# Halves of the neighbours' sums stored tile by tile, and step 1's adjacency products placed anew, in a four-layer graph kernel

## The chip, the cores and the metric

The kernel runs on one core of a Trainium2 chip. The metric is device time in microseconds (us) of one execution; less is better. The kernel before has a median of 3286.2 us over 14 runs (3276.45 to 3298.38).

Five engines work side by side, each through its own queue in order: TensorE (PE; matmuls, its weight loads shown as PEld), VectorE (DVE), ScalarE (ACT), GpSimd (POOL) and SyncE (SP). DMAs are issued from the queues of SP, ACT and POOL. They wait for one another by semaphores.

## What is computed

The input is x (4096 x 256) and a symmetric 0/1 adjacency `adj` (4096 x 4096, about 33 entries in a row). Four layers follow one another, each with a residual and a layer norm. The change lies in the second, which makes two steps:

```python
R = S + jnp.eye(N); R = R / R.sum(-1, keepdims=True)      # S is adj
Xf = X; Xa = X
for n in range(STEPS):                                    # two steps
    A = _top_p_attention(Xa, W1, W2, W3)                  # softmax, kept up to mass 0.9, normalised
    Xf = R @ Xf
    Xa = A @ Xa
    Z = Z + Xf @ U1[n].T + Xa @ U2[n].T
h = X + Z                                                 # then a layer norm
```

`R @ Xf` is the neighbours' sum: an adjacency product, a row sum and a scale. `A @ Xa` is attention. Layers one, three and four have one adjacency product each; the third also needs the number of two-way edges of each row.

## The kernel before

All rows are cut into 32 tiles of 128. Values that must keep their precision go through TensorE as two halves, an upper one of the leading bits and the rest; `split` (L145) makes them with three operations: L148 (VectorE, mask), L149 (ScalarE, copy of the upper half) and L150 (VectorE, subtraction). An adjacency product of one tile is 32 matmuls 128x512 over the halves of all tiles (`xh`, one buffer of the pool's tag "H") and one more for the diagonal (L683, L685 in `neighbours`); the adjacency comes as 8-bit pieces from `adj8_d` over SP's queue (L678) and is cast by ScalarE (L680). `r_end` (L700) scales the sum (L702, L703) and stores it in `xf_d` (L709). In step 0 the same loop also makes the two-way edge counts (L693, read at L707).

`run_step` (L941) is called for step 0 and step 1. Its loop runs i from -2 to 31. Iteration i makes the logits of tile i + 2 (L411, L412), searches the largest entries of tile i + 1 (L430, L525, L527), and multiplies tile i by its attention, then mixes (L819, L821). In step 0 a row keeps at most 16 entries: GpSimd gathers them (L669) and TensorE sums them (L758) with diagonal tiles (L756). In step 1 the whole row is turned (L741) and multiplied (L766). `pieces` (L720) runs the eight groups of a tile, and puts four matmuls of an adjacency product into each group if the iteration has one. Before the loop's first tile (i < 0) products are made by themselves (`r_product`, L711).

Which product belongs to which iteration: `FIRST` lists, for each step, the products of i = -2 and i = -1; each later iteration i makes product i + 2, if that is beyond FIRST's last. In step 0 that is 0 to 1, 2 to 3, then one in each iteration up to i = 29. In step 1, products 0 to 4 are made in the boundary between the steps (L1050), 5 to 7 in i = -2, 8 to 10 in i = -1, and 11 to 31 in i = 9 to 29, so that iterations 0 to 8 have none.

Rows whose kept mass needs more entries than were searched are set aside and done in extra tiles, "jobs" (`put_off`, L894): one in step 0, four in step 1, begun at i = 7, 15, 23 and 30 and moved on twice in each iteration, with five probes of a whole row (L495) in step 1. `left_over` (L921) is a loop for those beyond the jobs; all engines read its trip count (L926), which makes a barrier of it. In step 0 it stands in the last iteration. Behind the step's loop come the boundary's products, then `finish` of the job, whose flag (L585) is read back for a branch (L645).

The halves that step 1 needs are made in step 0's last iteration by `load_halves` (L152, called at L1026): eight loads of four tiles from `xf_d` over SP's queue into a scratch tile (the buffer of a logits tile), each followed by a split.

The order on each engine is not the order of the source: a scheduler of the framework arranges the instructions between two branches on each engine's queue. It already puts matmuls of later products ahead into iterations that have none. The text below calls the result the planned order; for the changed program it can be listed without running it.

Of the kernel before, what the change touches and what calls it, by code (L numbers as in the profile page):

```python
# [11 lines left out]
F32 = mybir.dt.float32  # L12
I32 = mybir.dt.int32
# [4 lines left out]
F32R = mybir.dt.float32r  # L18
# [6 lines left out]
P = 128  # L25
D = 256
# [28 lines left out]
def gnn_stack(ctx, tc, x, adjt, adjn, w0, b0, w1, w2t, w3t, u1t, u2t, ln_g, ln_b, w2, b2, w3, b3, out):  # L55
# [3 lines left out]
    nc = tc.nc  # L59
    N = x.shape[0]  # L60
    NT = N // P
    LC = min(512, N)
    NLC = N // LC
    JP = min(8, NT)
# [50 lines left out]
    zu_d = dram.tile([N + P, 2 * D], F32, name="zu_d")  # L115
    xa_d = dram.tile([N + P, D], F32, name="xa_d")
    xf_d = dram.tile([N, D], F32, name="xf_d")
    list_d = [dram.tile([N + P, 1], I32, name=f"list{n}_d") for n in range(STEPS)]

    adj8_d = [dram.tile([P, NT, P], F8, name=f"adj8_{it}_d") for it in range(NT)]  # L120
# [8 lines left out]
    def rows(t, it):  # L129
        return t[it * P : (it + 1) * P, :]  # L130

    def all_rows(t):
        return t.rearrange("(t p) d -> p t d", p=P)
# [18 lines left out]
    def load_halves(scratch, src, queue, cols=slice(None), ahead=2, copy=nc.scalar.copy):  # L152


        xh = hpool.tile([P, NT, 2 * D], F32R, tag="H", name="xh")
        W = J0 * D
        for c in range(NT // J0):
            s = slice(c * J0, (c + 1) * J0)
            t, up = (scratch[:, k * W : (k + 1) * W].rearrange("p (j d) -> p j d", d=D) for k in (c % ahead, ahead + c % 2))
            if queue is None:  # L160
                t = src[:, s, :]
            else:
                queue.dma_start(t, all_rows(src)[:, s, cols])
            split(up.bitcast(I32), xh[:, s, :], t, copy)
        return xh
# [186 lines left out]
    with tc.tile_pool(name="l1", bufs=1, reuse_waits="tile") as l1:  # L352
# [2 lines left out]


        FIRST = [[range(k * NT // 16, (k + 1) * NT // 16) for k in range(2)]]
        FIRST.append([range(5 * NT // 32, 8 * NT // 32), range(8 * NT // 32, 11 * NT // 32)])
        ones_sq = l1.tile([P, P], F32, name="ones_sq")
        nc.vector.memset(ones_sq, 1.0)  # L360

# [71 lines left out]
        QW = N // NQ  # L433

        spare_row = l1.tile([P, 4 * QW], U8, name="spare_row")
        no_e = spare_row[:, 4 * P : 4 * P + QW]

        def sparse(st):

# [260 lines left out]
        def r_end(i, acc_r, pn):  # L700
            xf_new = work.tile([P, D], F32, tag="xf_new", name="xf_new", bufs=1)
            nc.scalar.activation(xf_new, acc_r[:, :D], AF.Copy, scale=rs[:, i : i + 1])  # L702
            nc.vector.scalar_tensor_tensor(xf_new, acc_r[:, D:], rs[:, i : i + 1], xf_new, op0=ALU.mult, op1=ALU.add)  # L703
            if pn is not None:

                junk = spare_row.bitcast(F32)[:, :P]
                nc.vector.scalar_tensor_tensor(junk, pn[:, :P], 1.0, ident, op0=ALU.mult, op1=ALU.mult,  # L707
                                               accum_out=nef[:, i : i + 1])
            nc.sync.dma_start(rows(xf_d, i), xf_new)  # L709

        def r_product(n, i, xf):  # L711

# [228 lines left out]
        def run_step(n, es):  # L941

            later = {"base": spare0}
            tiles = {}
            last = []
            jobs = []

            def advance(job):  # L950

                cur["late"] = True
                st = next(job["stages"], "end")
                cur["late"] = False
                if st == "end":
                    return True
                if st is not None:
                    job["st"] = st
                return False

            def finish(job, last, todo=(), beside=()):
                while not advance(job):
                    for f in todo[:4]:
                        f()
                    todo = todo[4:]
                for f in todo:
                    f()
                ops = {}
                for k, f in enumerate(beside):
                    ops.setdefault(k * NLC // len(beside), []).append(f)  # L970
                for k, fs in enumerate(last):
                    ops.setdefault(k + 1, []).extend(fs)
                cur["late"] = True
                pieces(n, job["st"], None, ops)
                cur["late"] = False
                return [[f] for f in after(n, job["st"])]

            starts = {min((k + 1) * NT // LATER[n] - 1, NT - 2): k for k in range(LATER[n])}
            for i in range(-2, NT):
                st = tiles.pop(i, None)  # L980
                cd = tiles.get(i + 1)
                nxt = None
                if i + 2 < NT:

                    nxt = {"tile": i + 2, "q": cur["qs"].pop(0), "e": logits_in(es[i % 2]), "later": later, "G": {}}
                    tiles[i + 2] = nxt
                if i + 1 == NT and n == 0:
                    for fs in last:
                        for f in fs:
                            f()  # L990
                    last = []
                    left_over(n, es[NT % 2], later)
                ops = {}

                def at(g, f, *args):
                    ops.setdefault(g, []).append(lambda: f(*args))

                for g, fs in zip((1, 2), last):
                    for f in fs:
                        at(g, f)  # L1000
                if 0 < i + 2 < NT - 1:
                    turned = []
                    g = 1 if n else 6
                    at(g - 1, lambda i, turned: turned.append(transposed(cur["xa"][:, i + 3, :])), i, turned)
                    at(g, lambda turned: cur["qs"].append(query(None, turned[0])), turned)
                if cd is not None:
                    peak_groups(cd)
                    at(1, exp_rows, cd)
                for job in jobs:
                    at(1, advance, job)  # L1010
                if cd is not None:
                    rounds = 8 if n else KEPT // 8
                    at(2, tops, cd, rounds)
                    at(2, pick, cd, rounds)
                    at(4, flag, cd)
                    if n == 0:
                        for k in range(8):
                            at(4 + k // 2, gather, cd, k)
                    else:
                        at(5, lambda cd: [None for _ in settle(cd)], cd)  # L1020
                for job in jobs:
                    if n and i + 1 == NT:
                        at(4, advance, job)
                    at(6, advance, job)
                if i + 1 == NT and n == 0:
                    cur["next"] = load_halves(es[1 - NT % 2], xf_d, nc.sync)  # L1026
                if i < 0:
                    now = FIRST[n][i + 2]
                else:
                    now = [i + 2] if FIRST[n][1][-1] < i + 2 < NT else []  # L1030
                pieces(n, st, nxt, ops, now)
                last = [[f] for f in after(n, st)] if st is not None else []
                if i in starts:
                    k = starts[i]
                    if len(jobs) > (i == NT - 2):
                        last = finish(jobs.pop(0), last)
                    e = es[NT % 2] if k + 1 == LATER[n] else es[2]
                    jobs.append({"stages": put_off(n, k, e, later)})
                    if i < NT - 2:
                        advance(jobs[-1])  # L1040
            if n == 0:
                for fs in last:
                    for f in fs:
                        f()
                last = []
                cur["late"] = True
                fetch(n, jobs[0]["st"])
                cur["late"] = False
                cur["nef_done"] = True
                for i in range(FIRST[1][0][0]):  # L1050
                    r_product(1, i, cur["next"])
            todo = []
            if n > 0:

                z_room(es[1 - NT % 2])
                todo = [lambda i=i: zu_tile(i) for i in range(NT)]
            for k, job in enumerate(jobs):
                if k + 1 < len(jobs):
                    last = finish(job, last, beside=todo[: NT // 2])
                    todo = todo[NT // 2 :]  # L1060
                else:
                    last = finish(job, last, todo)
            for fs in last:
                for f in fs:
                    f()
            if n > 0:
                left_over(n, es[NT % 2], later)

        for n in range(STEPS):
            cur["n"] = n  # L1070
# [155 lines left out]
```

## Time and profile before

| what | us |
|---|---|
| median of 14 runs | 3286.2 |
| lowest, highest | 3276.45, 3298.38 |
| the profiled execution | 3294.68 |
| its span, first to last instruction | 3293.0 |
| TensorE busy in the span | 2976.4 (90%) |
| VectorE busy | 2291.4 (70%) |
| ScalarE busy | 1743.7 (53%) |
| GpSimd busy | 788.5 (24%) |

The stages in the span: layer one up to about 370 us, step 0 with its first products up to 1262, the boundary to 1418, step 1 to 2743, layers three and four to the end.

How to read the rows: a group of instructions shows its line, engine, operation, output<-inputs, shape and number, then busy time, mean ns of one, and the idle time of the engine just before them with what ended it. A timeline row shows start, length, engine, line, operation, tile, number of instructions, and in brackets the idle time before it and its releaser. A busy TensorE is not TensorE at its peak, since matmuls are pipelined and their ends are modelled. A wait for several semaphores is put down to the one that came last.

### The profile page before, as it was taken

How to read it: one execution, taken by the hardware profiler on the slowest of the kernel's cores; microseconds unless marked ns; L12 is line 12 of the kernel's file. 1: busy time of each engine (PE TensorE's matmuls, PEld its weight loads, DVE VectorE, ACT ScalarE, POOL GpSimd, SP SyncE). 2: the span in 40 equal slices, each digit the busy share in tenths (PEclk: the TensorE clock that was granted, in tenths of full speed). 3: DMA queues.
4: the chain of work that ended last, by engine and by line, in shares of the span. 5: the costliest groups of instructions: out<-in, count | busy, mean ns of one | idle time of the engine just before them, and what ended most of it. 6: DMA issues, size and time to landing. Idle time of an engine off the chain costs nothing. (4 is left out here: it accounts for less than half of the span.)

```text
span 3293.0 us, 45754 instructions
## 1 busy us (share of the span) xinstructions
PE 2976.4 (90%) x14376; PEld 2337.7 (71%) x14376; DVE 2291.4 (70%) x7161; ACT 1743.7 (53%) x2906; POOL 788.5 (24%) x915
## 2 busy tenths in 40 slices
PE   7999878999999996889989898989999796999998
PEld 3788656777777774668877777777787654888886
DVE  4666767787777885367988897888799673444444
ACT  3555545565555663465555454545465333666664
POOL 1111256666666664000000001000100001000000
PEclk9999989999999998989999999999999898999999
DMA  9995457777777775140001111011011134333332
GB/s 169 163 176 106 81 103 130 127 149 136 134 125 137 132 143 147 45 136 26 25 23 23 31 39 31 25 33 34 26 39 27 48 135 127 109 107 105 104 108 82
DMA packets 247872, 300.14 MB, mean 91 GB/s; under 512 B 34688, under 2 KB 201536, under 8 KB 247616
## 3 DMA queue, kind: packets, MB, share of 16 engines
q0 software_dynamic: 46576, 104.94, 23.1%
q1 hardware_dynamic: 188800, 180.93, 18.6%
q10 hardware_dynamic: 12240, 11.23, 1.1%
q8 instruction: 116, 1.90, 0.2%
q14 instruction: 140, 1.15, 0.2%
HBM read 331.17 MB, written 66.45 MB: 121 GB/s over the span
## 5 line engine op out<-in xcount | busy, mean ns | idle before, releaser
L683 PE MATMUL acc_r<-xh,adjq 128*128 128x512 f32 x2048 | 612.4, 430 | 39.2 <-ACT adjq L680 22.2
L766 PE MATMUL acc_bank<-xa,at 128*128 128x256 f32 x2304 | 570.3, 388 | 34.4 <-ACT at L744 33.9
L669 POOL DMA_INDIRECT G<-x_d,cols x512 | 500.0, 977 | 292.5 <-PE acc_bank L758 118.8
L680 ACT CAST adjq<-adj 128x512 fp32r<-128x512 fp8e4 x512 | 316.3, 620 | 404.6 <-PE acc_r L683 197.3
L766 PEld LDWEIGHTS acc_bank<-xa,at 128*128 128x128 f32 x2304 | 425.2, 194 | 96.3 <-ACT at L744 45.0
L683 PEld LDWEIGHTS acc_r<-xh,adjq 128*128 128x128 f32 x2048 | 377.8, 192 | 138.7 <-ACT adjq L680 49.2
L412 ACT COPY e<-lg 128x512 f32<-128x512 f32 x552 | 320.4, 587 | 241.6 <-PE lg L411 201.2
L430 DVE MAX8 cand<-e 128x8 f32<-128x256 f32 x1024 | 383.1, 415 | 74.7 <-ACT e L412 42.7
L197 POOL TENSOR_TENSOR rstd<-ve,mhalf 128x1 f32<-128x1 f32 x168 | 103.4, 615 | 1352.7 <-DVE ve L195 1287.9
L411 PE MATMUL lg<-kS,q 128*128 128x512 f32 x1104 | 401.6, 449 | 10.8 <-issue 5.4
L1106 ACT CAST a<-a 128x1024 fp32r<-128x1024 fp8e4 x256 | 267.9, 1048 | 157.5 <-PE acc L173 121.3
L758 PE MATMUL acc_bank<-G,dg 128*128 128x256 f32 x1024 | 286.8, 399 | 38.2 <-DMA G<-x_d,cols 15.9
L527 DVE FIND_INDEX8 cols<-top,e 128x8 uint32<-128x4096 f32 x64 | 282.8, 4419 | 0.0
L173 PE MATMUL acc<-xh,a 128*128 128x512 f32 x1024 | 255.7, 403 | 21.6 <-DMA a<-adj_d 15.8
L758 PEld LDWEIGHTS acc_bank<-G,dg 128*128 128x128 f32 x1024 | 196.6, 197 | 93.5 <-DMA G<-x_d,cols 26.5
L173 PE MATMUL acc<-y0h,a 128*128 128x512 f32 x1024 | 253.7, 400 | 0.0
L173 PEld LDWEIGHTS acc<-xh,a 128*128 128x128 f32 x1024 | 191.6, 190 | 64.9 <-ACT xh L149 24.1
L173 PE MATMUL acc<-yh,a 128*128 128x512 f32 x1024 | 233.7, 390 | 0.0
L744 ACT COPY at<-at_ps 128x512 f32<-128x512 f32 x296 | 173.7, 589 | 101.5 <-PE at_ps L741 100.2
L173 PEld LDWEIGHTS acc<-yh,a 128*128 128x128 f32 x1024 | 192.1, 188 | 39.7
L173 PEld LDWEIGHTS acc<-y0h,a 128*128 128x128 f32 x1024 | 188.0, 188 | 42.2 <-issue 0.6
L411 PEld LDWEIGHTS lg<-kS,q 128*128 128x128 f32 x1104 | 185.8, 195 | 34.5 <-ACT e L412 13.4
(287 smaller groups left out, 4519.4 us busy)
## 6 DMA issues: line engine op xcount, KB each, us to landing
adj<-adj_d SPq DMA_DIRECT2D x256, 128.0 KB
a<-adj_d SPq DMA_DIRECT2D x256, 128.0 KB
a<-in_adjt POOLq DMA_DIRECT2D x64, 256.0 KB
adj_d<-a SPq DMA_DIRECT2D x64, 256.0 KB
adjn<-in_adjn POOLq DMA_DIRECT2D x64, 256.0 KB
x_d<-x SPq DMA_DIRECT2D x64, 128.0 KB
xf_d<-xf_new SPq DMA_DIRECT2D x64, 128.0 KB
G<-x_d,cols POOLq DMA_INDIRECT x512
```

What stands on the lines that cost most here:

```text
L173: nc.tensor.matmul(acc, a[:, j, :], halves(jt), start=(jt == 0), stop=(jt == NT - 1))
L411: nc.tensor.matmul(pl[:, :LC], q[k], kS[:, s], start=(k == 0), stop=(k == 1))
L412: nc.scalar.copy(l[:, s], pl[:, :LC])
L430: nc.vector.max(dst[:, 8 * g : 8 * g + 8], src[:, g * GW : (g + 1) * GW])
L527: nc.vector.max_index(st["at"][:, 8 * r : 8 * r + 8], t8, st["e"][:, :N])
L669: nc.gpsimd.indirect_dma_start(out=g, out_offset=None, in_=x1_d, in_offset=bass.IndirectOffsetOnAxis(ap=st["at"][:, k : k + 1], axis=0))
L680: nc.scalar.copy(a, cur["a8"][:, g % 2 * GP : (g % 2 + 1) * GP, :])
L683: nc.tensor.matmul(acc_r, a[:, j, :], xf[:, jt, :], start=(jt == 0), stop=False)
L744: nc.scalar.copy(at[:, :G, :], ps[:, :G, :])
L758: nc.tensor.matmul(acc_a, dg[:, k % 4, :], st["G"][k], start=(k == 0), stop=(k == KEPT - 1))
L766: nc.tensor.matmul(acc_a, ats[g][:, j, :], cur["xa"][:, jt, :], start=(jt == 0), stop=(jt == NT - 1))
L1106: nc.scalar.copy(a, a8)
```

## The change

A new tensor `xh_d` (4096 x 512) in device memory takes the halves. In step 0, `r_end` splits each tile's sum as soon as it is made (L148 to L150 on one tile, 128x256, through a strip of `spare_row`) and stores the halves over SP's queue; `xf_d` is stored as before. The exponentials' unused output `no_e` moves behind that strip. `load_halves` at the end of step 0 is replaced by four loads of eight tiles each, straight into the operand, issued behind iteration 29. The scratch tile is no longer used for it.

In step 1, products 0 to 8 belong to the boundary: five where they were, two behind the job's `finish`, two behind its mix. Products 9, 10 belong to i = -2 and 11, 12 to i = -1. The other nineteen, 13 to 31, are spread evenly over i = 0 to 28.

```diff
+    xh_d = dram.tile([N, 2 * D], F32, name="xh_d")
...
-        FIRST.append([range(5 * NT // 32, 8 * NT // 32), range(8 * NT // 32, 11 * NT // 32)])
+        FIRST.append([range(9 * NT // 32, 11 * NT // 32), range(11 * NT // 32, 13 * NT // 32)])
+        BETWEEN = (5, 7, 9)
...
-        no_e = spare_row[:, 4 * P : 4 * P + QW]
+        no_e = spare_row[:, 4 * (P + D) : 4 * (P + D) + QW]
...
             nc.sync.dma_start(rows(xf_d, i), xf_new)
+            if pn is not None:
+
+                xh = cur["w"].tile([P, 1, 2 * D], F32R, tag="xh_new", name="xh_new", bufs=1)
+                up = spare_row.bitcast(I32)[:, P : P + D]
+                split(up[:, None, :], xh, xf_new[:, None, :])
+                nc.sync.dma_start(rows(xh_d, i), xh[:, 0, :].bitcast(F32))
...
-                if i + 1 == NT and n == 0:
-                    cur["next"] = load_halves(es[1 - NT % 2], xf_d, nc.sync)
                 if i < 0:
                     now = FIRST[n][i + 2]
+                elif n == 0:
+                    now = [i + 2] if FIRST[n][1][-1] < i + 2 < NT else []
                 else:
-                    now = [i + 2] if FIRST[n][1][-1] < i + 2 < NT else []
+                    a = FIRST[n][1][-1] + 1
+                    b, c = (min(a + k * (NT - a) // (NT - 3), NT) for k in (i, i + 1))
+                    now = range(b, c)
                 pieces(n, st, nxt, ops, now)
                 last = [[f] for f in after(n, st)] if st is not None else []
+                if n == 0 and i == NT - 3:
+                    cur["next"] = xh = hpool.tile([P, NT, 2 * D], F32R, tag="H", name="xh")
+                    for c in range(NJP):
+                        s = slice(c * JP, (c + 1) * JP)
+                        nc.sync.dma_start(xh[:, s, :].bitcast(F32), all_rows(xh_d)[:, s, :])
...
-                for i in range(FIRST[1][0][0]):
+                for i in range(BETWEEN[0]):
                     r_product(1, i, cur["next"])
...
+            if n == 0:
+                for i in range(BETWEEN[0], BETWEEN[1]):
+                    r_product(1, i, cur["next"])
             for fs in last:
                 for f in fs:
                     f()
             if n > 0:
                 left_over(n, es[NT % 2], later)
+            else:
+                for i in range(BETWEEN[1], BETWEEN[2]):
+                    r_product(1, i, cur["next"])
```

## The prediction

> **What bounds the kernel now.** The chain of waits that ended last lies almost wholly in the two last layers, which the change leaves alone, so I read it only to know that, and then took the busy time stage by stage. Columns: stretch, length, busy us (instructions) of TensorE, its weight loads, VectorE, ScalarE, GpSimd, granted clock, DMA share, GB/s.
>
> ```profile
> 441.00:1262.00 821.00, 739.31 (x3978) 574.19 (x3978) 634.96 (x1864) 461.42 (x895) 529.94 (x558) 0.97 0.74 133
> 1262.00:1330.00 68.00, 41.72 (x145) 29.55 (x144) 32.58 (x77) 21.45 (x35) 27.09 (x26) 0.75 0.47 129
> 1368.00:1418.00 50.00, 29.60 (x140) 24.05 (x139) 13.95 (x28) 8.57 (x19) 2.92 (x3) 0.76 0.41 124
> 1418.00:1507.00 89.00, 85.66 (x387) 65.85 (x386) 58.70 (x185) 59.55 (x102) 1.95 (x2) 0.96 0.27 70
> 1507.00:1705.00 198.00, 189.17 (x998) 158.75 (x997) 178.33 (x613) 105.17 (x176) 15.85 (x21) 1.00 0.08 24
> 1705.00:2571.00 866.00, 798.82 (x3972) 657.45 (x3970) 740.33 (x2433) 449.82 (x748) 67.53 (x82) 0.97 0.14 30
> ```
>
> To be seen: step 0 (first row) has no engine full; the boundary (second and third row) leaves TensorE idle a third of the time; the head of step 1 (fourth) and its first seven tiles (fifth) belong to TensorE; the rest of step 1 (sixth) has VectorE at 85% and TensorE at 92%. Single iterations say it more sharply:
>
> ```profile
> 1535.00:1563.00 28.00, 26.73 (x142) 22.46 (x141) 25.42 (x88) 15.03 (x25) 2.24 (x3) 1.00 0.08 24
> 2414.00:2448.00 34.00, 32.83 (x169) 27.26 (x168) 33.05 (x113) 18.37 (x33) 2.23 (x3) 1.00 0.12 35
> 1845.00:1888.00 43.00, 36.45 (x175) 29.64 (x174) 34.88 (x115) 21.24 (x37) 2.23 (x3) 0.96 0.25 35
> ```
>
> The first has TensorE back to back (its timeline shows idle stretches of 1.10 and 0.18 us only). The second carries a whole adjacency product and the probes of a set-aside job: VectorE is full. The third carries the same and lasts 43 us with neither full: there one waits for the other. What VectorE waits for after 1705, from the view of waits (us in total, times, longest):
>
> ```profile
> DVE h L821 <- PE mm_bank L819: 36.2, 10, 7.9
> DVE xf_new L703 <- ACT xf_new L702: 9.3, 2, 6.4
> DVE thr L455 <- ACT e L453: 7.6, 2, 5.9
> ```
>
> These 53.1 us are what adjacency products ahead of other work cost there. In the boundary, the timeline of TensorE:
>
> ```profile
> 1293.96 2.04 PE L683 MATMUL acc_r<-xh,adjq 128*128 128x512 f32 x4 [10.57 <-DVE xh L150]
> 1304.29 3.78 PE L758 MATMUL acc_bank<-G,dg 128*128 128x256 f32 x8 [6.05 <-DMA adj<-adj_d]
> 1343.87 7.91 PE L683 MATMUL acc_r<-xh,adjq 128*128 128x512 f32 x32
> 1367.91 0.19 PE L585 MATMUL mm_bank<-ones_col,bad_l 128*1 128x1 f32 x2
> 1376.26 1.97 PE L741 MATMUL at_ps<-ident,e 128*128 128x128 f32 x8 [8.15 <-DVE e L660]
> ```
>
> TensorE waits for halves that VectorE makes from loads, gets through the loop's barrier (about 1301), does five products, and only then the flag (L585) of a job whose data were ready at 1340.5 (L561 on VectorE). A product is 33 matmuls: 1343.87 to 1351.85, 7.98 us, 0.242 us each.
>
> **The sum's frame.** The profiled execution took 3294.7 us (span 3293.0 and 1.7 around it), 8.5 above the median 3286.2. I sum the differences and apply them to the median.
>
> **Step 0, new work per tile.** The last layers make the same halves of one tile: L148 and L150 (128x256) take 0.295 and 0.411 us on VectorE, L149 0.401 on ScalarE. 32 tiles: 22.6 us VectorE, 12.8 ScalarE, and 32 stores of 256 KB on SP's queue (8 MB in 821 us, 10 GB/s on top of 133). What hides them: VectorE idles 186 us of the 821, ScalarE 360. In the planned order of the changed program the subtraction stands ahead of the second index search, which feeds gathers and the flag; SP issues the new store ahead of the store of h, which comes no earlier anyway, so the loads of adjacency queued behind wait little longer. GpSimd's gathers feel such work:
>
> ```profile
> 1309.92 0.95 POOL L669 DMA_INDIRECT G<-x_d,cols  x1 [0.30 <-issue]
> 1312.44 1.56 POOL L669 DMA_INDIRECT G<-x_d,cols  x1 [0.30 <-issue]
> 1314.31 1.27 POOL L669 DMA_INDIRECT G<-x_d,cols  x1 [0.30 <-issue]
> 1311.95 1.23 DVE L150 TENSOR_TENSOR xh<-e 128x1024 fp32r<-128x1024 f32 x1
> ```
>
> Beside these two operations a gather takes 1.27 to 1.56 instead of 0.95. One such hit per tile is 0.3 us, 10 us in all. The Trainium skill speaks against this part of the change: in "SBUF — State Buffer", section "Who interferes with whom", VectorE in a two-port mode locks GpSimd out for the whole instruction, and with two SBUF inputs it collides with a GpSimd operation that reads SBUF. By that page each tile could hold GpSimd up for both operations, an estimate of 23 us in all; by the rows above it is 10.
> Bounds: 0 (all in idle time) to +32 (22.6 and 10, all on the path). GpSimd spends 530 of 821 us busy and about 140 waiting for TensorE, so a small delay mostly shortens a wait: I take **+6**.
>
> **The boundary.** Gone: eight loads with a split each, 8 x 1.92 us VectorE and 8 x 1.05 ScalarE, tied to one scratch tile. In their place four loads of 2 MB straight into the operand. The first can start after the last matmul of tile 31's product (about 1256), the others when tile 31's halves are stored (about 1266). 6 MB at the stage's 129 GB/s take 47 us; 1400 to 1415 moved 325 GB/s, which gives 19. In the planned order TensorE does one whole product ahead of the barrier, with the end of tile 30 behind its first chunks, so the barrier follows the last chunk by some 2 us: 1287 to 1315 against 1298. I take 1297. Behind the barrier VectorE no longer stands before the diagonal tiles (2.95 us for a load, then four splits), so gathers and logits come some 7 us earlier; 131 product matmuls instead of 149 stand before the flag, 18 x 0.242 = 4.4. Flag: 13 us earlier. Behind it 37 matmuls (8.9 us) fill the wait of 8.15. Then 93 more (22.5 us) stand among the end of the job's sum, its mix, the first queries and the keys' transposes (1396 to 1414), where TensorE now waits 11.5 us; the first transposes and sums after the wait, run at half speed now (1.97 and 3.33 us instead of 1.0 and 1.89), save 2.4. 22.5 - 11.5 - 2.4 - (1.6 not on the path, as the keys' loads wait for the mix) = +7. Sum -13 + 7 = **-6**, bounds -18 (loads at 325, no product on the path) to +12 (loads at 129).
>
> **Head of step 1.** 132 product matmuls instead of 198 stand before the end of tile 0: 66 x 0.242 = **-16**; -10 if tile 1's data (ready 1485) come late.
>
> **First seven tiles.** The planned order puts 160 product matmuls there, 57 before. TensorE is full: 103 x 0.242 = **+25**. VectorE's 178 of 198 us can't help; the only cover is some 1.3 us of wait per tile, so +17 at least.
>
> **The later tiles.** 467 instead of 636, 169 fewer: 41 us of TensorE, all gained if TensorE set the pace, nothing if VectorE does (33.05 of 34 us). Nearest row: the 53.1 us that VectorE waits behind products, in proportion, 53.1 x 169/636 = **-14**. Bounds -41 to 0.
>
> **Sum:** 6 - 6 - 16 + 25 - 14 = -5, so **3281** on the median.
>
> **Rivals.**
> *VectorE holds the later tiles* (the other side). If iterations such as 2414 to 2448 set the pace, the 14 don't come: +9, 3295. For it: 33.05 of 34. Against it: the 43 us iteration. It decides once 1705 to 2571 shrinks by less than 2 us (then the sum is +7).
> *Step 0 pays in full.* +32 instead of +6: +21, 3307. For it: the chain search, gathers, sum has no long slack; against it: 186 us idle on VectorE.
> *The halves come late.* With 6 MB at 129 GB/s the barrier is 18 us later than taken: +13, 3299. Against it: 325 GB/s was reached.
> *TensorE paces the later tiles after all.* All 41 come: -32, 3254. For it: TensorE at 92% there.
> That the products are not really moved is excluded by the planned order; the plan already hoisted eight matmuls of later products into each early tile, which the counts hold.
>
> **How the numbers follow.** Chances: forecast 0.42 (own range 3268 to 3292: 0.19 of it under -0.2%, 0.19 within, 0.04 above), VectorE 0.18 (0.04 of it within), step 0 0.13, late halves 0.07, TensorE 0.20. The range reaches to the outer rivals, 3254 to 3308. A measurement of this kernel tells about 0.2%, 6.6 us. Faster 0.19 + 0.20 = 0.39; same 0.19 + 0.04 = 0.23; slower 0.04 + 0.14 + 0.13 + 0.07 = 0.38.
>
> **What would show it.** Step 0: 441 to 1262 longer by 6, gathers longer. Boundary: no idle time before L683 for L150; L585 near 1355; transposes right behind products. Seven tiles of 28.2 us turn into 28 to 34. The later tiles: waits of L821 for L819 well under 36 us. A barrier after 1315, or a step 0 over 20 us longer, makes the forecast wrong; so does an even spread that TensorE cashes in fully.

## The result, and the profile after

The changed kernel is slower: median 3314.5 us of 10 runs (lowest 3305.17) against 3286.6 us of the kernel before (47 runs, 3276.12 to 3307.54); ratio 1.0076, 95% interval 1.006 to 1.0093. One of the ten took 13216.48 us, four times as long as the others, for a reason that nothing here shows; it does not count in the ratio. By the ratio the change costs 25 us; 3281 were forecast, and the range ended at 3308. The profiled execution took 3321.5 us (span 3319.8). Lines of the changed kernel lie a little further down: L685 is the product's matmul (L683 before), L766 the gathered sum (L758), L829 the mix's sum (L821), L587 the flag (L585), L1108 the keys' transposes (L1087), L810 the load of xf (L802).

The six stretches that the prediction showed, in the changed kernel, between the same events; columns as there.

```profile
433.60:1268.00 834.40, 748.69 (x4012) 578.30 (x4011) 650.82 (x1963) 475.54 (x928) 523.42 (x561) 0.97 0.77 140
1268.00:1341.00 73.00, 47.87 (x157) 34.02 (x157) 18.44 (x62) 16.12 (x32) 24.75 (x26) 0.70 0.62 186
1378.00:1447.00 69.00, 58.82 (x268) 45.75 (x267) 15.08 (x37) 28.31 (x53) 2.92 (x3) 0.93 0.39 124
1447.00:1527.50 80.50, 69.95 (x323) 54.70 (x324) 56.87 (x183) 49.08 (x84) 2.75 (x2) 0.94 0.23 61
1527.50:1751.10 223.60, 213.15 (x1100) 178.11 (x1098) 181.31 (x618) 120.37 (x205) 15.78 (x21) 1.00 0.12 30
1751.10:2593.70 842.60, 763.55 (x3805) 627.91 (x3803) 733.05 (x2432) 426.82 (x701) 70.79 (x83) 0.96 0.12 28
```

To be seen: the stretch from the flag to the first logits is 69.0 us, 50 before; the first seven tiles 223.6, 198 before, with VectorE as busy as it was (181.3, 178.3) and so idle for 42 us instead of 20; the later tiles 842.6, 866 before.

Cut finer, by events found in each trace (first transposes of the job's row, flag, scaling of the job's sum, first transpose of keys, scaling of tile 0, of the 8th, 33rd and last sum of step 1), in us, with the kernels that the next sections explain:

| stretch | before | after | old spread | places only | halves only | none behind flag | from iteration 0 |
|---|---|---|---|---|---|---|---|
| step 0, tiles 0 to 29 | 804.1 | 817.5 | 778.3 | 786.3 | 783.8 | 800.5 | 794.7 |
| to the job's row | 66.2 | 71.1 | 69.5 | 67.2 | 69.1 | 66.2 | 66.4 |
| to the flag | 49.5 | 48.6 | 48.4 | 52.2 | 48.6 | 48.3 | 48.3 |
| to the job's sum | 28.2 | 31.0 | 29.0 | 27.6 | 31.0 | 30.8 | 31.1 |
| to the keys' transposes | 17.8 | 36.8 | 37.5 | 37.0 | 18.4 | 15.9 | 36.4 |
| to the end of tile 0 | 92.8 | 81.8 | 82.8 | 82.4 | 92.7 | 109.8 | 87.7 |
| first seven tiles | 198.0 | 223.6 | 197.7 | 223.0 | 197.8 | 197.7 | 240.9 |
| later tiles | 866.4 | 842.7 | 842.3 | 840.7 | 859.3 | 833.5 | 832.5 |
| to the last sum | 163.2 | 167.5 | 161.8 | 167.3 | 163.7 | 164.1 | 165.3 |

Layer one and step 0 together take 1212 to 1258 us in these traces, whatever the kernel, so step 0 is read through timed ratios, and the other rows as they stand. "First seven tiles" are iterations 1 to 7; the later tiles are iterations 8 to 30, with two of the jobs. Later tiles with 570 product matmuls in them took 832.5 to 846.4 in ten kernels' executions; a difference under 14 us there is not read.

### The profile page after: what moved, and what is told of

The parts are those of the page before. It is cut to its first block, busy times and chain, and to the rows that moved or that the text cites. A ratio compares the mean times of both kernels' runs of the same rounds, so it can differ in the third digit from the quotient of the medians.

```text
span 3319.8 us, 45981 instructions
## 1 busy us (share of the span) xinstructions
PE 2986.0 (90%) x14376; PEld 2342.2 (71%) x14376; DVE 2288.4 (69%) x7209; ACT 1750.4 (53%) x2930; POOL 780.2 (24%) x915
## 5 line engine op out<-in xcount | busy, mean ns | idle before, releaser
L685 PE MATMUL acc_r<-xh,adjq 128*128 128x512 f32 x2048 | 611.6, 431 | 35.6 <-ACT adjq L682 20.4
L774 PE MATMUL acc_bank<-xa,at 128*128 128x256 f32 x2304 | 569.8, 388 | 22.6 <-ACT at L752 22.3
L685 PEld LDWEIGHTS acc_r<-xh,adjq 128*128 128x128 f32 x2048 | 379.2, 193 | 139.9 <-ACT adjq L682 57.8
L414 ACT COPY e<-lg 128x512 f32<-128x512 f32 x552 | 321.0, 586 | 223.6 <-PE lg L413 183.0
L766 PE MATMUL acc_bank<-G,dg 128*128 128x256 f32 x1024 | 287.7, 400 | 45.2 <-DMA G<-x_d,cols 38.9
L766 PEld LDWEIGHTS acc_bank<-G,dg 128*128 128x128 f32 x1024 | 195.4, 197 | 102.3 <-DMA G<-x_d,cols 47.8
L186 ACT COPY xt<-tr 128x256 f32<-128x256 f32 (+1 forms) x268 | 112.1, 426 | 207.6 <-PE tr L184 170.9
```

Of the source, the lines that this page charges most:

```text
L414: nc.scalar.copy(l[:, s], pl[:, :LC])
L685: nc.tensor.matmul(acc_r, a[:, j, :], xf[:, jt, :], start=(jt == 0), stop=False)
L766: nc.tensor.matmul(acc_a, dg[:, k % 4, :], st["G"][k], start=(k == 0), stop=(k == KEPT - 1))
L774: nc.tensor.matmul(acc_a, ats[g][:, j, :], cur["xa"][:, jt, :], start=(jt == 0), stop=(jt == NT - 1))
```

## Experiments

After the two traces my theory was A: the boundary makes the loss (a load held behind 6 MB, products that hide nothing), and the even spread only moves work. Its rivals were B, step 0's new work, and C, the even spread itself. The kernel before ran on the same chip as each kernel, with medians of 3259.7 to 3283.4 us; ratios to it are given.

### The old spread

```diff
-                elif n == 0:
+                else:
                     now = [i + 2] if FIRST[n][1][-1] < i + 2 < NT else []
-                else:
-                    a = FIRST[n][1][-1] + 1
...
```

> The changed kernel with one edit taken back: the products 13 to 31 of step 1 come one per iteration in iterations 11 to 29, as before, not spread over all iterations. Theory A (the boundary makes the loss; the spread only moves TensorE's work from the later tiles into the first ones): the first seven tiles go back to 28.3 us each (-25 us), the later ones get the 24 us back that they had given, so 3314 within 5 us, ratio to before 1.006 to 1.009. Theory C (the even spread makes the loss, because TensorE is full in the first tiles and the later tiles, held by VectorE, give less back): 15 us or more faster than the changed kernel, 3300 or less, ratio under 1.004.

Measured 0.997 (0.9956 to 0.9984), faster than before and in theory C's range. Theory A fell on its main point: taking back the spread alone turns 25 us of loss into 10 of gain. The two kernels' stretches differ by 25.9 us in the first seven tiles, 0.4 in the later ones and 5.7 behind them. The rows of this kernel for the first seven and the later tiles:

```profile
1481.50:1679.20 197.70, 189.13 (x998) 158.71 (x997) 178.56 (x614) 105.07 (x176) 15.81 (x21) 1.00 0.08 24
1679.20:2521.50 842.30, 777.33 (x3908) 644.72 (x3906) 741.45 (x2442) 437.16 (x731) 69.77 (x82) 0.97 0.11 30
```

The 104 product matmuls (25 us of TensorE) that stand in these later tiles and not in those of the changed kernel cost nothing: 842.3 against 842.6. This is one execution of each; the scatter of 14 us stated above is its limit.

### Stores alone, halves alone, places alone

The kernel with stores has `r_end`'s new lines on the kernel before, and nobody reads them. The one with halves is the changed kernel with all products at their old places. The one with places is the change without stores and with the old `load_halves`. Of the edits, the products' old places in the kernel with halves, which also takes back the spread as above:

```diff
-        FIRST.append([range(9 * NT // 32, 11 * NT // 32), range(11 * NT // 32, 13 * NT // 32)])
-        BETWEEN = (5, 7, 9)
+        FIRST.append([range(5 * NT // 32, 8 * NT // 32), range(8 * NT // 32, 11 * NT // 32)])
+        BETWEEN = (5, 5, 5)
...
```

> The kernel before with the stores of step 0 alone: every tile's halves are made and stored, and nobody reads them; loads, products and their places are those of before. Theory A (boundary): step 0 pays 6 us as in the prediction, the rest is unchanged: 3290 to 3295, ratio 1.001 to 1.0025. Theory B (the stores make the loss: 22.6 us of VectorE, 12.8 of ScalarE and 8 MB more on SP's queue, all on step 0's path): 3306 or more, ratio 1.006 or more. Theory C (spread): 3287 to 3293.

Measured 1.0006 (0.9994 to 1.0019): +2 us, 0 within the interval. B falls. The 32 subtractions take 13.0 us on VectorE and the 32 copies 13.2 on ScalarE, and no more than the interval's 6 us of it can lie on the path.

> Halves stored in step 0 and loaded in four loads, but all products where they were: five in the boundary, six before tile 0, one per iteration from 9 on. Theory A (boundary): step 0 +6, and the load of tile 30's xf waits in SP's queue behind 6 MB of halves, which makes the barrier and the set-aside job about 5 to 11 us late, while behind the flag nothing changes: 3297 to 3304, ratio 1.003 to 1.0055. Theory B (stores): 3306 or more, and the kernel with stores alone already as slow. Theory C (spread): under 3293.

Measured 1.0006 (0.999 to 1.0021), under A's range and in C's. In the boundary it is 5.8 us longer than the kernel with stores (167.1 against 161.3 from step 0's tile 29 to the keys), and 8 shorter in the later tiles, which is inside their scatter.

> The kernel before with the products' new places alone (nine in the boundary, four before tile 0, the rest spread evenly); halves are loaded and split in the boundary as before, nothing is stored in step 0. Theory A: step 0 unchanged; barrier near before's 1301; behind the flag about 20 us more, as 90 product matmuls fill little of the 11 us that TensorE waits there; before tile 0 11 to 16 less; seven tiles +25, later ones -24: +10 to +17, 3297 to 3304, ratio 1.003 to 1.005. Theory B (stores): within 3 us of before. Theory C (spread): +20 or more, 3307, with the sum of the first seven and the later tiles 15 us or more longer.

Measured 1.0048 (1.003 to 1.0067), inside A's range and under C's: against the kernel before, the first seven and the later tiles together are not 15 us longer but 0.7 shorter (223.0 + 840.7, 198.0 + 866.4), since this kernel also has two products fewer in step 1's iterations. C holds against the old spread, not against the kernel before. Its stretches repeat those of the changed kernel to 2 us from the keys' transposes on: most of the loss comes from places. The boundary is 3.5 us shorter than in the changed kernel (184.0 against 187.5). By time the halves could account for 0.0028, 9 us, with intervals that overlap; the stretches from step 0 on show no more than the 3.5.

### Nine products in the boundary, old spread, nothing stored

```diff
-                nc.sync.dma_start(rows(xh_d, i), xh[:, 0, :].bitcast(F32))
...
+                if i + 1 == NT and n == 0:
+                    cur["next"] = load_halves(es[1 - NT % 2], xf_d, nc.sync)
```

> Nine products in the boundary and the old spread, but halves loaded and split as before, nothing stored in step 0. Theory V (the even spread makes the loss and two products fewer in the later tiles the gain; the stored halves move nothing): like the kernel with the old spread and stored halves, ratio 0.996 to 0.999. Rival (the stored halves make that kernel's gain): 1.000 or more.

Measured 0.9951 (0.9931 to 0.9972), a little under V's range and far from the rival's 1.000; theory V is worked out in the next section. With the kernel of places alone (1.0048) it differs in the spread only: 0.0097, 32 us; with the stored halves it was 1.0076 against 0.997, 35 us. Twice the same price for the spread, and no gain from halves.

### The spread by dose

The price of the spread led to theory V: the iterations up to 7 of step 1 have no set-aside job in work, so in each of their 28.0 us VectorE has 25.4 us of work and TensorE is busy for 26.7 (the first single iteration that the prediction showed). A product there adds to TensorE and makes VectorE wait; the later iterations are paced by VectorE, which works through probes and settling of jobs there, so TensorE's lighter load is not cashed in.

```diff
-                    b, c = (min(a + k * (NT - a) // (NT - 3), NT) for k in (i, i + 1))
-                    now = range(b, c)
+                    now = [i + a] if i + a < NT else []
```

> The changed kernel with products 13 to 31 one per iteration from iteration 0 to 18. Theory V (the whole of tiles 0 to 31 costs VectorE's work plus its idle time; a product in an early iteration, which has no set-aside job, only makes VectorE idle, and the later tiles are held by VectorE and give little back): the first seven tiles 35 to 37 us each, +56 on 198; the later ones 815 to 842; ratio 1.009 to 1.016, slower than the changed kernel (1.0076). Rival (each product costs its 8 us of TensorE wherever it stands): later tiles 790 or less, ratio within 0.003 of the changed kernel's or better.

Measured 1.0122 (1.009 to 1.0154), as V said; the seven tiles took less than I had written (240.9, not 254), as 231 matmuls stand in them and not 288.

```profile
1506.80:1747.70 240.90, 229.73 (x1170) 191.51 (x1169) 183.14 (x622) 130.62 (x225) 15.71 (x21) 1.00 0.12 35
1747.70:2580.20 832.50, 735.79 (x3706) 612.65 (x3704) 733.34 (x2429) 405.91 (x674) 71.65 (x83) 0.95 0.11 26
```

With 367 product matmuls the later tiles take 832.5, inside the 832.5 to 846.4 that they take with 570: 203 matmuls, 49 us of TensorE, and no gain that shows. VectorE is busy for 733 to 742 us there in every kernel. The granted clock is lower there too (0.95, against 0.97 under the old spread), so a slower TensorE could have eaten the gain. Five iterations, 19 to 23, settle that: from iteration 0 (first row) they hold 4 product matmuls, under the old spread (second row) 171.

```profile
2166.20:2337.30 171.10, 134.11 (x680) 112.14 (x679) 165.47 (x560) 71.15 (x118) 13.65 (x15) 0.89 0.06 17
2090.20:2266.30 176.10, 167.35 (x846) 138.92 (x845) 164.66 (x558) 95.12 (x164) 14.17 (x15) 0.99 0.15 36
```

167 matmuls, 40 us of TensorE, bring 5.0 us. VectorE (third pair) is busy for 165.5 of 171.1 us in the first row while TensorE idles for 37: in these iterations VectorE sets the pace, whatever the clock. Two iterations of the changed kernel show both sides: the first is early and holds a whole product, the second late and holds none.

```profile
1716.70:1751.10 34.40, 32.81 (x169) 27.35 (x167) 25.32 (x88) 18.67 (x33) 2.24 (x3) 1.00 0.11 32
2540.00:2571.80 31.80, 26.77 (x131) 22.38 (x130) 30.94 (x109) 13.45 (x22) 2.86 (x4) 0.89 0.06 17
```

In the first VectorE (third pair) works 25.32 of 34.40, in the second 30.94 of 31.80, with TensorE five us idle. The same iteration takes 32.0 us under the old spread, with 33 product matmuls in it.

Not every late iteration is like this one. In the changed kernel iteration 18 holds no product and takes 24.6 us, 34.3 under the old spread; but iterations 19 and 20 hold 44 and 41 product matmuls and take 42.4 and 44.3 us, against 33.9 each with 33, and VectorE idles for 6 and 10 us of them. The job's work shifts between iterations, and gains and losses cancel. How much the even spread would bring without such bunches no run here shows.

What VectorE waits for in the first seven tiles, first in the kernel before, then in the changed one (us, times, longest):

```profile
DVE cand L430 <- ACT e L412: 3.9, 6, 0.7
```

```profile
DVE cand L432 <- ACT e L414: 25.8, 14, 2.9
```

It is the search of the next tile's logits; they come later, presumably because product matmuls stand between their own on TensorE.

> The changed kernel with products 13 to 31 one per iteration from iteration 7 to 25. Theory V: the first seven tiles 28.3 us each as before; the later tiles within 8 us of the 842 that they take with products in 11 to 29, as VectorE holds them: ratio 0.995 to 0.9995. Rival (it is the place within the later tiles that counts, beside jobs or not): the later tiles over 10 us away from 842.

Measured 0.9982 (0.9955 to 1.0008); seven tiles 197.5, later ones 841.0. As V said: in the later tiles it makes no difference that shows whether the products begin in iteration 7 or 11.

### What stands in the boundary

First the wait at the barrier. The load of xf for tile 30's mix to ScalarE's queue, old spread:

```diff
-                    nc.sync.dma_start(st[key], rows(src, i))
+                    q = nc.scalar if n == 0 and i == NT - 2 else nc.sync
+                    q.dma_start(st[key], rows(src, i))
```

> The kernel with the old spread (0.997 of before), with the load of tile 30's xf issued on ScalarE's queue, not on SP's behind the four loads of halves. Theory A (that load holds the barrier: TensorE waits 15.1 us for it at the barrier): the set-aside job's gather and its flag come 5 to 11 us earlier and all behind them too, ratio 0.9935 to 0.9955. Rival (the halves themselves or the adjacency tiles of the first product end last there anyway): the wait goes to a product matmul, the gather moves by under 3 us, ratio 0.996 to 0.998.

The wait in the changed kernel, TensorE's timeline and below it SP's:

```profile
1286.48 3.75 PE L685 MATMUL acc_r<-xh,adjq 128*128 128x512 f32 x8 [2.20 <-DMA xh<-xh_d]
1304.75 0.69 PE L184 MATMUL tr<-ident,xf 128*128 128x128 f32 x2 [14.52 <-DMA xf<-xf_d]
```

```profile
1273.67 0.32 SPq L717 DMA_DIRECT2D xh_d<-xh_new  x1
1274.04 8.43 SPq L1047 DMA_DIRECT2D xh<-xh_d  x3
1282.57 6.79 SPq L810 DMA_DIRECT2D xf<-xf_d  x1
```

Three loads of halves, 6 MB, go out at 1274.04 behind the store of the last tile's halves; the small load behind them lands at 1304.75. Measured 0.9962 (0.9941 to 0.9982), the rival's range, though the interval reaches into both; the job's row comes 3.8 us earlier (65.7 against 69.5), most of it lost again up to the flag (51.4 against 48.4), and the wait has another name in that kernel:

```profile
1287.17 0.80 PE L685 MATMUL acc_r<-xh,adjq 128*128 128x512 f32 x1 [15.51 <-ACT adjq L682]
```

ScalarE waits 18.82 us there for a store of keys whose buffer it writes next, and 0.68 more for an adjacency tile; both stand behind the same loads in SP's queue. Then two of the four loads behind the barrier:

```diff
-                    for c in range(NJP):
+                    for c in range(2):
...
                     left_over(n, es[NT % 2], later)
+                    for c in range(2, NJP):
+                        s = slice(c * JP, (c + 1) * JP)
+                        nc.sync.dma_start(cur["next"][:, s, :].bitcast(F32), all_rows(xh_d)[:, s, :])
```

> The kernel with the old spread (0.997 of before; 0.9962 with tile 30's xf on another queue), with only the first two loads of halves ahead of the barrier and the other two behind it. Theory A' (whatever stands behind 6 MB of halves in SP's queue is late, a load of xf in one kernel, an adjacency tile in the other, and holds the barrier by about 15 us): the gather of the set-aside job comes 5 to 12 us earlier against the end of step 0, ratio 0.992 to 0.995. Rival (the loads then hold the products ahead of the flag, which are TensorE's work all the same): gather earlier, flag not, ratio 0.996 to 0.999.

Measured 0.9945 (0.9925 to 0.9966), in the range of theory A', with an interval that reaches into the rival's; the job's row 6.3 us earlier (63.2), a third of it lost again up to the flag (50.6 against 48.4). The wait got a third name, VectorE's:

```profile
1288.88 0.69 DVE L764 TENSOR_TENSOR dg<-ident,w 128x512 f32<-128x512 f32 x1 [14.08 <-DMA xh<-xh_d]
```

A wait of 14 to 15.5 us under three names, each time released by what came with or behind the halves; before, TensorE waited 10.57 for a split and 6.05 at the barrier. So the loads of halves hold the barrier, and took the splits' place. Loads that stay out of the barrier altogether were not tried.

Then what stands behind the flag. Five products in the boundary instead of nine, old spread:

```diff
-        FIRST.append([range(9 * NT // 32, 11 * NT // 32), range(11 * NT // 32, 13 * NT // 32)])
-        BETWEEN = (5, 7, 9)
+        FIRST.append([range(5 * NT // 32, 9 * NT // 32), range(9 * NT // 32, 13 * NT // 32)])
+        BETWEEN = (5, 5, 5)
```

> The kernel with the old spread, with five products in the boundary, not nine: none behind the flag, eight before tile 0, from 13 on as there. Theory A (products behind the flag take 22 us there, and 32 us of TensorE when they stand before tile 0): boundary 22 us shorter, the stretch before tile 0 about 25 to 32 longer, sum +3 to +10, ratio 0.998 to 1.000. Rival (they only stand in the way of the keys' loads, which wait behind their adjacency tiles on SP's queue, and TensorE has room before tile 0): sum -5 to -15, ratio 0.9925 to 0.9955.

Measured 0.9999 (0.9978 to 1.0021), A's range: 21.6 us less ahead of the keys' transposes, 27.0 more behind them. Four products, 32 us of TensorE, cost 22 us behind the flag (nothing up to the job's sum, 29.0 with them and 30.8 without) and 27 ahead of tile 0: the place gains 5 us. The rival said that the keys' loads were in the way: in the changed kernel they stand behind adjacency tiles in SP's queue, as its timeline shows, with TensorE's below:

```profile
1424.05 0.32 SPq L405 DMA_DIRECT2D xq<-xa_d  x1
1424.46 0.42 SPq L810 DMA_DIRECT2D res<-h_d  x1
1424.98 13.44 SPq L680 DMA_DIRECT2D adj<-adj_d  x4
1438.99 0.32 SPq L711 DMA_DIRECT2D xf_d<-xf_new  x1
1439.36 1.02 SPq L1105 DMA_DIRECT2D e<-k_d  x2
```

```profile
1427.82 0.66 PE L184 MATMUL tr<-ident,xq 128*128 128x128 f32 x2 [5.80 <-DMA xq<-xa_d]
...
1437.43 8.21 PE L685 MATMUL acc_r<-xh,adjq 128*128 128x512 f32 x32
...
1445.71 1.03 PE L1108 MATMUL kt_ps<-ident,e 128*128 128x128 f32 x8
```

The keys' loads were issued 11.7 us behind the job's sum before (1407.83), 30.5 here (1439.36). But the transposes at 1445.71 follow a product without a gap. To tell loads from products:

```diff
-                nc.sync.dma_start(t, rows(src, i))
+                nc.gpsimd.dma_start(t, rows(src, i))
...
-                        nc.sync.dma_start(k_rows[:, s, :], all_rows(k_d[:N, :])[:, s, :])
+                        nc.gpsimd.dma_start(k_rows[:, s, :], all_rows(k_d[:N, :])[:, s, :])
```

> The kernel with the old spread, with the loads of the first two queries' rows and of the keys issued on GpSimd's queue, which is idle there, so that no adjacency tile stands ahead of them. Theory Q (the 37 us between the job's mix and the keys' transposes, 18 before, come from SP's queue, where those loads wait behind the adjacency tiles of products 5 to 8): TensorE's waits of 5.8 and 2.9 us for them go, and mix to end of tile 0 gets 6 to 12 us shorter than 120, ratio 0.993 to 0.9955. Rival W (TensorE's own work: 92 product matmuls of 0.24 us stand there, and the order that TensorE follows, not the loads, sets it): under 4 us shorter, ratio 0.996 to 0.998.

```profile
1420.04 6.00 POOL L1101 DMA_DIRECT2D e<-k_d  x8 [1.84 <-DMA k_d<-kt,to_l]
```

```profile
1421.90 0.66 PE L184 MATMUL tr<-ident,xq 128*128 128x128 f32 x2 [7.18 <-DMA xq<-xa_d]
...
1441.13 0.60 PE L1104 MATMUL kt_ps<-ident,e 128*128 128x128 f32 x4
```

TensorE's wait for the second query rows, which theory Q had going away, is 7.18 us (5.80 in the changed kernel). The keys' loads go out 17.6 us behind the job's sum, 13 sooner than in the changed kernel, and their transposes still come when TensorE is through with the products: the stretch to them is 38.8 us (37.5 without the edit), that to tile 0's end 79.0 (82.8). Together 2.5 us: the rival W by the stretch. By time it is 0.9927 (0.9905 to 0.9949), just under theory Q's range, and 6 us of the gain lie at the very end: GpSimd's last instruction, a drain that waits for its queue, takes 2.63 us in this kernel and 8.76 in all that leave those loads on SP's queue and add no transfer.

> Both edits in one kernel: two loads of halves behind the barrier, query rows and keys on GpSimd's queue, old spread. If each gives what its theory says, they add up, as they lie on the same chain: ratio 0.988 to 0.993. If neither does: 0.996 to 0.998.

Measured 0.9928 (0.9905 to 0.9952): at the edge of the range that stood for adding up, yet no faster than the keys' edit alone. By stretches, from step 0's tile 29 to the end of tile 0, the loads' edit gains 4.8 us on the old spread, the keys' edit 1.9 and both 5.6, so most of it adds up there; differences of this size can't be told by time. Its last drain is 2.63 as well. This kernel and the last one are the fastest found, both faster than the kernel before.

> The kernel with the old spread, with ten small transfers more on GpSimd's queue (128 rows of one number each, written to a place that nobody reads, in the last iterations of step 1), 745 GpSimd transfers in all instead of 735, as many as the kernel with query rows and keys on that queue has. If that kernel's gain at the very end (GpSimd's last drain took 2.63 us there and 8.76 in all others) comes from the number of transfers and not from the keys: the drain is 2.63 again, ratio about 0.002 under the 0.997 of the old spread, and of the 0.9927 of the keys' kernel as much is not the keys' doing. If it comes from where the keys' loads stand: the drain is 8.76, ratio 0.997.

> The same with four transfers more, 739 in all. If the last drain goes by the number of transfers in small steps: between 2.63 and 8.76 us, some 6.3 by a straight line; if by a threshold between: one of the two.

The drain took 9.57 with ten transfers more and 9.08 with four: 0.081 us for each beyond 735. So it is not their number that makes it short; those loads themselves do, in a way that no run here shows. The first of the two kernels ran at 1.0015 (0.9996 to 1.0035), not at 0.997. Its edit lies at the end of step 1, its stretches from the job's row on are like those of the kernel that it was made from, or shorter (later tiles 832.6, to the last sum 162.7); layer one and step 0 up to tile 29 took 1257 us in its profile (1212 to 1258 in the others). What lengthened these is open, and with it differences of 0.004 between kernels that were not timed side by side. The verdict on the spread (0.0097 and 0.0106, and by stretches 25 and 32 us) is beyond that; 0.9927 against 0.997 is not.

## Why the prediction was wrong, step by step

The span grew by 26.8 us: step 0 and what lies before it +6.0, boundary up to the keys' transposes +25.8, head -11.0, seven tiles +25.6, later ones -23.7, end +4.3.

- **Step 0, +6:** that the one execution gives +6.0 is luck: step 0 itself, the stretch that the prediction named, is 13.4 us longer (834.4 against 821.0), and what lies before it 7.4 shorter, among stretches that scatter by 46 us. The timed kernel with stores alone says +2 (-2 to +6). The rows that were to show it do not: a gather took 0.966 us on average, 0.974 before, and 11 of 466 took over 1.2 us, 20 of 462 before. By the Trainium skill's page "SBUF — State Buffer", section "Who interferes with whom", I had worked out an estimate of 23 us for VectorE holding GpSimd up; no such delay is to be seen in the gathers. "Step 0 pays in full" falls.
- **The boundary, -6: the step that failed.** It measured +26, and its miss of 32 us is as large as that of the whole sum in these executions (+26.8 for -5): the other terms' errors, +5, -10 and +4, happen to cancel. Two terms of it: "Flag: 13 us earlier" became 4 later, counted from the end of step 0, since the barrier did not come at 1297 but at about 1317 (1311 without step 0's 6), on the trace's own scale past the 1315 that the prediction had named as a sign of its being wrong; I had four loads run ahead of it at up to 325 GB/s, and had not counted what is queued behind 6 MB on SP (a load of xf, a store of keys, adjacency tiles). And "+7" for the products behind the flag became 22 (2.8 up to the job's sum, 19.0 from there to the keys): I set 11.5 us of TensorE's waits against them, and its idle time there fell from 11.4 only to 8.0, since the waits for the query rows stayed between the products. "The halves come late" had the mechanism, at a price of 18 us on the barrier, but not the second half.
- **Head, -16:** -11.0; TensorE's idle time there grew from 4.1 to 10.8 us, since it waits 7.3 for adjacency tiles that ScalarE casts (3.0 before) and 3.3 between the keys' transposes for the keys' loads. "-10 if tile 1's data come late" had the size, with another wait.
- **Seven tiles, +25:** +25.6, by the term's own count of matmuls.
- **Later tiles, -14:** -23.7, and for another reason. I shared the gain over all 169 matmuls by proportion. The experiments say that the first 66 (two products moved to the boundary) bring all of it, 864 on average with 636 matmuls (three kernels) and 840 with 570 (ten), and that 104 to 203 more bring nothing that shows. From the kernel before to the old spread 22.3 of the 24.1 us lie in iterations 11 to 15 (208.9 to 186.6 us), which hold 223 product matmuls before and 126 under the old spread, 101 of them before in iteration 15 alone: there the 97 matmuls, 23.5 us of TensorE, count almost in full. "VectorE holds the later tiles" was the mechanism; its sign, "once 1705 to 2571 shrinks by less than 2 us", could not show it, as the two parts of the change were mixed in one number. "TensorE paces the later tiles" falls.
- **Signs:** waits of L829 for L827 fell from 36.2 to 21.6 us, as said. VectorE's idle time from tile 0 to the last sum is the better account: its work is 1019 to 1021 us in the kernel before, the changed one, the old spread and that from iteration 0, and its idle time 208, 213, 183 and 217.

The two accounts fit together. With the old spread the boundary costs 23 us as well, and the head and the later tiles, with two products fewer in step 1's iterations, give 34 back: so that kernel gains (10 us by time, 16 without stores). The even spread then loses 32 to 35 us against it; my sum, which took the seven tiles and the later ones together at +11 (25 - 14), did not separate the two.

## What to carry over

When work is moved from a stretch where two engines take turns to one where a single engine is full, the price is paid whole and the return is what the other engine leaves: count the other engine's work in both stretches (here VectorE, 25.4 us of 28.0 early, 30.9 of 31.8 late) ahead of sharing a gain by proportion. Idle time in front of a row of short waits is not room for a long block: ask which waits stay between its pieces. And a transfer moved earlier has to be charged with what stands behind it in its queue: here loads of 6 MB, and a wait of 14 to 15.5 us.

## What was not expected of the hardware

GpSimd's drain at the end of the kernel took 8.76 us in twelve kernels with 735 GpSimd transfers, 9.08 with 739 and 9.57 with 745, all on the end of the time; with ten plain loads of query rows and keys on that queue, 745 as well, it took 2.63. Moving those loads gave 6 us at a place that has nothing to do with them.
